# Layer 0's attention weights: GpSimd's image additions placed behind its products, score sums ordered by column tiles, the skips' matrix made with the softmax

## The chip, the core and the metric

The kernel runs on one core of a Trainium2 chip. The core has five engines with a queue of instructions each: TensorE (PE in the profile: matmuls; PEld are its weight loads), VectorE (DVE), ScalarE (ACT), GpSimd (POOL) and SyncE (SP, which here only issues DMAs). Engines wait for each other through semaphores. Operands lie in SBUF, matmul results in PSUM, both with 128 partitions; GpSimd's operands in this kernel are all in SBUF. The metric is the device time of one execution in microseconds (us); lower is better.

## The reference, cut to what matters

Two layers run on x of shape (4, 32, 128, 128): 4 batches of 32 images of 128 x 128. Layer 0, the only one touched, is a Fourier-space attention between the 32 images of a batch, with 32 heads, and two spectral convolutions behind it:

```python
k = _fno_layer(xn, Kcw, Ksw, Hs, Ws)
q = _fno_layer(xn, Qcw, Qsw, Hs, Ws)
v = _fno_layer(xn, Vcw, Vsw, H, W)
...
scores = jnp.einsum('bntk,bnsk->bnts', qf, kf) / (np.float32(np.sqrt(Hs * Ws)) * temperature)
p_attn = jax.nn.softmax(scores, axis=-1)
av = jnp.einsum('bnts,bnsk->bntk', p_attn, vf)
p = _fno_layer(av, Pcw, Psw, H, W)
a = _inorm(p + xa, attn_w, attn_b)
an = _inorm(a, norm2_w, norm2_b)
m = _fno_layer(an, m0cw, m0sw, H, W, inner_norm=True, act=True)
m = _fno_layer(m, m1cw, m1sw, H, W, inner_norm=True, act=False)
out = _inorm(m, mon_w, mon_b) + a
```

K, Q and V are spectral convolutions of one-channel images, so a head's score of two images is a weighted sum, over spectral positions, of products of the two images' spectra. The kernel makes those products once for all heads and lets TensorE weigh and sum them. `p_attn`, the probabilities, then mix the images, and `_fno_layer`'s skip terms mix them by a 32 x 32 matrix per batch (the "skips' matrix").

## The kernel before

The program is written in Tile: engines and tiles are chosen by hand, the framework puts in the semaphores and orders each engine's instructions. It does so ahead of time by a schedule of its own: program order is priority, but an instruction that its estimate takes to be ready is put ahead of one that it takes to be waiting. Tiles with the same tag share a fixed number of buffers, and a tile waits until a buffer is free. Within one PSUM bank the writes of one tile keep the order of the program.

Layer 0 loops over the 4 batches (L702). For batch b it mixes the spectra by the probabilities, works through the two convolutions, and near the end prepares batch b + 1: normalization and spectra (`image_sums`, `spectra_of_images`), then `attention_weights(b + 1, front)` (L1009). Batch 0's weights are made ahead of the loop (L648). So there are four executions of `attention_weights`, one after another in time, each followed by the mixing stage of its batch.

`attention_weights` (L489 to L595):

- The spectra `xx` of the 32 images are copied into `xe`, `xm` (SBUF) and `xp` (PSUM). TensorE sums the diagonal terms (`so`), VectorE spreads them into `sod` (L518).
- The product loop runs over 17 columns yy. Each makes `pa` and `pb`, 128 x 544 products of every image with its 16 neighbours (and itself) around the circle of 32. `pa` is always VectorE's (L534); `pb` is VectorE's in odd columns and GpSimd's in even ones (L536). TensorE multiplies them by the heads' weights (L540, L542) and sums over columns in `sp`, in four strips of 32 PSUM partitions: `pa` or `pb`, even or odd column.
- `sod`, `pa`, `pb`, and later `spt`, `ex` and `ph`, share tag `pr` with 6 buffers. The mixing stage's `u` products use the same tag.
- ScalarE copies `sp` to `spt` (L544). TensorE sums the scores `sc` in two halves of 16 images: for each half, in turn, `sod` (L552), the strips (L553), the mirrored strips (L555) and the column at distance nought (L558).
- Softmax: `mx`, `less` on VectorE, `ex` on ScalarE (L566), `sm`, `ph` on VectorE (L574). `ph` goes through DRAM (`prd`) into another layout (`pr`), by DMAs of the SP and ScalarE queues.

The main loop then makes the skips' matrix `bd` (L713 to L731): two matmuls `cm` (L718, tag `a`) of `ph` with `pv`, two products `cd` (L720, tag `v`, 3 buffers), two sums `cp` (L721), and two small operations. `pv` and `psw2` are loaded by four small DMAs and multiplied (L693 to L699), behind the loads of the two convolutions' weights.

The mixing stage (L766 to L803) loads the spectra again (`xb`, L773), copies them to PSUM on ScalarE (`xw`, L782), multiplies on VectorE (L790) and GpSimd (L788) into `u`, and sums on TensorE (`po`, L793). The skips (`pxt` L738, `sk` L757) stand between.

The end of a batch (L1010 to L1031): ScalarE scales the 32 images of `gl` (L1014). GpSimd adds `gl` to `xr` in four additions of 8 images (L1021). The inverse transform `back` (matmuls L297, evacuations into tag `v` by L187 and L189, matmuls L308) ends in VectorE's `last` (L1025), which adds to the same `xr`; `xr` is then stored (L1031). In program order this comes behind `attention_weights(b + 1)`. In time the schedule mixes the two: ScalarE's L1014 and GpSimd's L1021 run inside the product loop of batches 1 to 3.

Of the kernel before, what the change touches and what calls it, by code (L numbers as in the profile page):

```python
# [7 lines left out]
F32 = mybir.dt.float32  # L8
# [5 lines left out]
P = 128  # L14
# [94 lines left out]
def layer0(  # L109
# [67 lines left out]
    ]  # L177
    grp, small = (p.__enter__() for p in work)
    pools += work

    flip = [0]

# [303 lines left out]
    def steps(a, *dims):  # L486
        return bass.AP(tensor=a.tensor, offset=a.offset, ap=[a.ap[0], *dims])

    def attention_weights(b, front):  # L489

        xx, (xe, xm), _ = front
        xs = per_image("xs")
        nc.vector.tensor_copy(xs, xx[:, :, 0])
        half = T // 2
        nd = half + 1


        xp = ps.tile([P, 2, 512], F32, name="xp", tag="wide")
        for r in range(2):
            y0, y1 = 9 * r, min(KA, 9 * r + 9)  # L500
            nc.scalar.copy(
                xp[:, r, : (y1 - y0) * (T + half)].rearrange("p (y t) -> p y t", t=T + half), xe[:, y0:y1]
            )


        tt = [P, T, nd]
        twice = [P, 2, T]
        so = ps.tile([T, 2, T], F32, name="so", tag="wide")
        xh = per_image("xh")
        nc.vector.tensor_scalar(xh, xs, 0.5, None, ALU.mult)  # L510
        for yy in range(KA, 32):
            x_y = xx[:, :, 1 + KY + yy]
            nc.tensor.matmul(
                so, x_y, x_y.unsqueeze(1).to_broadcast(twice), start=yy == KA, stop=False
            )
        nc.tensor.matmul(so, xh, xs.unsqueeze(1).to_broadcast(twice), start=False, stop=True)
        sod = grp.tile([T, T, T], F32, name="sod", tag="pr", bufs=6)
        nc.vector.tensor_tensor(  # L518
            sod,
            ident[:T, :T].unsqueeze(2).to_broadcast([T, T, T]),  # L520
            steps(so, [1, T], [1, T]),
            ALU.mult,
        )

        sp = ps.tile([P, T, half], F32, name="sp", tag="b")
        sp0 = ps.tile([2 * NH, T], F32, name="sp0", tag="a")
        for yy in range(KA):
            row = xp[:, yy // 9, yy % 9 * (T + half) :]
            pa = grp.tile(tt, F32, name="pa", tag="pr", bufs=6)
            pb = grp.tile(tt, F32, name="pb", tag="pr", bufs=6)  # L530
            for k, t in enumerate((pa, pb)):
                other = (xm[:, yy] if k else xe[:, yy, :T]).unsqueeze(2).to_broadcast(tt)
                if k == 0 or yy % 2 == 1:
                    nc.vector.tensor_tensor(t, steps(row, [1, T], [1, nd]), other, ALU.mult)  # L534
                else:
                    nc.gpsimd.tensor_tensor(t, steps(xe[:, yy], [1, T], [1, nd]), other, ALU.mult)  # L536
            turn = dict(start=yy < 2, stop=yy >= KA - 2)
            for k, (wt, pp) in enumerate(((w_re, pa), (w_im, pb))):
                r = 32 * (2 * k + yy % 2)
                nc.tensor.matmul(sp[r : r + 32], wt[:, yy], pp[:, :, 1:], **turn)  # L540
            r = 32 * (yy % 2)
            nc.tensor.matmul(sp0[r : r + 32], w_re[:, yy], pa[:, :, 0], **turn)  # L542
        spt = grp.tile([P, 2, T, half], F32, name="spt", tag="pr", bufs=6)
        nc.scalar.copy(spt, sp.unsqueeze(1).to_broadcast([P, 2, T, half]))  # L544
        spt0 = small.tile([2 * NH, T], F32, name="spt0", tag="ym")
        nc.vector.tensor_copy(spt0, sp0)
        nn = [2 * NH, half, T]
        sc = ps.tile(nn, F32, name="sc", tag="wide")
        for h in range(2):
            i = slice(half * h, half * h + half)  # L550
            o = sc[32 * h : 32 * h + 32]
            nc.tensor.matmul(o, qk, sod[:, i], start=True, stop=False)  # L552
            nc.tensor.matmul(o[:, :, 1:nd], both_plus, spt[:, 0, i], start=False, stop=False)  # L553
            first = spt.rearrange("p r t d -> p (r t d)")[:, (half * h + nd) * half + half - 2 :]
            nc.tensor.matmul(  # L555
                o[:, :, nd:], plus_minus, steps(first, [half, half], [half - 1, half - 1]), start=False, stop=False
            )
            nc.tensor.matmul(o[:, :, 0], both_plus[: 2 * NH], spt0[:, i], start=False, stop=True)  # L558


        mx = small.tile([2 * NH, half], F32, name="mx", tag="mx")
        nc.vector.tensor_reduce(mx, sc, AX.X, ALU.max)
        less = grp.tile(nn, F32, name="less", tag="v", bufs=3)
        nc.vector.tensor_tensor(less, sc, mx.unsqueeze(2).to_broadcast(nn), ALU.subtract)
        ex = grp.tile([2 * NH, half, 2, T], F32, name="ex", tag="pr", bufs=6)
        nc.scalar.activation(ex, less.unsqueeze(2).to_broadcast([2 * NH, half, 2, T]), AF.Exp)  # L566
        sm = small.tile([2 * NH, half], F32, name="sm", tag="mx")
        nc.vector.tensor_reduce(sm, ex[:, :, 0], AX.X, ALU.add)
        nc.vector.reciprocal(sm, sm)
        ph = grp.tile([2 * NH, T, half], F32, name="ph", tag="pr", bufs=6)  # L570
        for h in range(2):
            r = slice(32 * h, 32 * h + 32)
            first = ex.rearrange("n t r d -> n (t r d)")[r, T - half * h :]
            nc.vector.tensor_tensor(  # L574
                ph[r],
                steps(first, [1, T], [2 * T - 1, half]),
                sm[r].unsqueeze(1).to_broadcast([32, T, half]),
                ALU.mult,
            )

        prd = dram.tile([2, T, 16, T], F32, name=f"prd_{b}")
        pr = big.tile([P, 4, 2, T], F32, name=f"pr_{b}", tag="prob")
        for k in range(2):
            for h in range(2):
                eng = nc.scalar if h else nc.sync
                p0 = 32 * h + 16 * k
                eng.dma_start(
                    out=prd[k, :, :, 16 * h : 16 * h + 16].rearrange("s n t -> n s t"),
                    in_=ph[p0 : p0 + 16],
                )  # L590
            eng = nc.scalar if k else nc.sync
            eng.dma_start(
                out=pr[:, :, k], in_=prd[k].rearrange("(i s) n t -> (s n) i t", i=4)
            )
        return ph, pr  # L595

    value_weights()
    normed = image_sums(0, loaded)
# [46 lines left out]
    pools.append(tc.tile_pool(name="l0_big", bufs=1))  # L645
    right.append(tc.tile_pool(name="l0_xb", bufs=4, side="right"))
    big, late = (p.__enter__() for p in (pools[-1], right[-1]))
    weights = attention_weights(0, front)  # L648


    layers = []
# [38 lines left out]
            nc.vector.memset(c0[r : r + 1, 2:4], 0.0)  # L690
        layers.append((w[:, 0], turned, (en, c0[:, 2:3]), (sq, c0[:, 3:4]), c0))

    pv = const.tile([2 * NH, 1], F32, name="pv")  # L693
    nc.sync.dma_start(out=pv[:NH], in_=heads[:, 2:3])
    nc.sync.dma_start(out=pv[NH:], in_=heads[:, 2:3])
    psw2 = const.tile([2 * NH, 1], F32, name="psw2")
    nc.sync.dma_start(out=psw2[:NH], in_=heads[:, 3:4])
    nc.sync.dma_start(out=psw2[NH:], in_=heads[:, 3:4])
    nc.vector.tensor_mul(pv, pv, psw2)  # L699


    for b in range(B):  # L702
        xt = loaded
        by_group, _, _, ysc = normed
        xd = front[2]
        if b + 1 < B:
            loaded = load(b + 1)

        ph, pr = weights

        cp = per_image("cp")  # L713
        sel = scalars(ALU.mult, "sel", same, ysc)
        for h in range(2):
            r = slice(32 * h, 32 * h + 32)
            cm = ps.tile([P, T, 16], F32, name="cm", tag="a")
            nc.tensor.matmul(cm, pv[r].to_broadcast([NH, P]), ph[r], start=True, stop=True)  # L718
            cd = grp.tile([P, T, 16], F32, name="cd", tag="v", bufs=3)
            nc.vector.tensor_tensor(cd, cm, sel.unsqueeze(2).to_broadcast([P, T, 16]), ALU.mult)  # L720
            nc.vector.tensor_reduce(  # L721
                cp[:, 16 * h : 16 * h + 16], cd.rearrange("p s t -> p t s"), AX.X, ALU.add
            )
        nc.vector.tensor_add(cp, cp, same)
        bd = small.tile([P, 4, T], F32, name="bd", tag="bd")
        nc.vector.tensor_tensor(
            bd,
            block.unsqueeze(2).to_broadcast([P, 4, T]),
            cp.unsqueeze(1).to_broadcast([P, 4, T]),
            ALU.mult,  # L730
        )  # L731
        q = big.tile([P, T, C], F32, name=f"q_{b}", tag="q")

        def skips(c0):
# [271 lines left out]
        nc.vector.tensor_mul(dg, dg, c3)  # L1006
        nc.vector.tensor_tensor(cq, cq, dg, ALU.add)
        if b + 1 < B:
            weights = attention_weights(b + 1, front)  # L1009
        for a in HALVES:  # L1010
            groups = [slice(16 * a + g, 16 * a + g + GI) for g in (0, GI)]
            for i in groups:
                for t in range(i.start, i.stop):
# [4 lines left out]
                        bias=cq[:, t : t + 1],  # L1018
                        scale=c2[:, t : t + 1],
                    )  # L1020
                nc.gpsimd.tensor_tensor(xr[:, i], xr[:, i], gl[:, i], ALU.add)  # L1021

            def last(images, four):
                for j, t in enumerate(images):
# [636 lines left out]
```

## Time and profile before

| | |
|---|---|
| median of 3 runs | 3184.4 us (3181.8 to 3186.39) |
| the profiled execution | 3176.48 us, its span 3174.4 us |
| mean granted TensorE clock | 0.954 of full |
| busy in the span | TensorE 92%, ScalarE 73%, VectorE 71%, GpSimd 65% |
| product loops of batches 0, 1, 2, 3 | 23.1, 26.4, 27.7, 27.7 us |

Times of the profile count from the span's start. A line of the timeline holds start, duration, engine, line of the program, operation, output and inputs with their shapes, how often, and in brackets the idle time of the engine just before and what ended it. In a table by stretches a number with (x) is the busy time of an engine and its instructions. "issue" is time in which an engine waited for nothing that the profile shows. TensorE takes each float32 matmul as two instructions, so counts of its rows are doubled. The end of a matmul is modelled.

### The profile page before, as it was taken

The page shows a single profiled execution, that of the slowest core. Times are in us where ns is not written, and L with a number is a line of the kernel's source. Part 1 is how long each engine was busy: PE and PEld are TensorE (multiplying, and loading weights), DVE is VectorE, ACT ScalarE, POOL GpSimd, SP SyncE. Part 2 cuts the span into 40 slices and gives each one's busy share as a digit, 9 for nine tenths or more (in the row PEclk, how much of TensorE's full clock was granted, in tenths as well). Part 3 has the DMA queues.
Part 4 walks back from the last instruction along what each step waited for, and adds up shares of the span by engine and source line. Part 5 has one row for each costly group of instructions (what it writes and reads, how often), then busy time and mean ns, then how long its engine had stood idle before and what let it go on. Part 6 is the DMA issues. An engine that isn't in the chain of part 4 may idle for free.

```text
span 3174.4 us, 52863 instructions
## 1 busy us (share of the span) xinstructions
PE 2911.8 (92%) x19530; PEld 1437.6 (45%) x19530; DVE 2257.4 (71%) x5054; ACT 2318.2 (73%) x3142; POOL 2053.0 (65%) x1819
## 2 busy tenths in 40 slices
PE   7888889798888789999999999999999999999997
PEld 4366366355446444444344444443444444444443
DVE  5776676667578557777666868866778776777887
ACT  2444343354354589998999999998999999999992
POOL 1621440350270388878888797889878889888773
PEclk8898898799798799999999999999999999999998
DMA  6401310220130201010111010021010011101000
GB/s 139 120 10 30 107 39 22 72 82 1 38 124 1 66 23 31 9 29 7 31 37 24 14 24 14 7 46 29 17 37 1 14 37 24 37 1 31 14 14 14
DMA packets 152306, 112.74 MB, mean 36 GB/s; under 512 B 36878, under 2 KB 140657, under 8 KB 151441
## 3 DMA queue, kind: packets, MB, share of 16 engines
q1 hardware_dynamic: 136209, 103.61, 12.3%
q10 hardware_dynamic: 15840, 5.77, 0.8%
q8 instruction: 154, 2.52, 0.3%
q14 instruction: 103, 0.84, 0.1%
HBM read 68.37 MB, written 20.00 MB: 28 GB/s over the span
## 4 chain that ended last, share of the span: by engine, by line
PE 62%; POOL 12%; ACT 9%; DVE 8%; issue 6%; DMA 2%; SPq 0%; POOLq 0%; DVEq 0%; ACTq 0%
PE d L1461 19%; PE po L1480 11%; PE px L1367 6%; ACT r L1511 5%; PE po L793 4%; PE n L1461 3%; POOL e L1520 3%; POOL e L1519 3%; PE pz L248 2%; PE four L308 2%; ACT e L1527 2%; PE px L886 2%; POOL kx L1126 1%; PE sk L757 1%; DVE r L1516 1%
## 5 line engine op out<-in xcount | busy, mean ns | idle before, releaser
L1516 DVE TENSOR_TENSOR r<-n,r 128x1024 f32<-128x1024 f32 (+1 forms) x1056 | 962.0, 953 | 478.3 <-PE n L1461 393.4
L1519 POOL TENSOR_TENSOR e<-r 128x512 f32<-128x512 f32 x528 | 673.0, 1275 | 268.7 <-DVE r L1516 268.1
L1511 ACT ACTIVATE r<-d 128x1024 f32<-128x1024 f32 (+1 forms) x1056 | 792.8, 802 | 68.8 <-PE n L1461 59.0
L1523 ACT ACTIVATE r<-r 128x1536 f32<-128x1536 f32 x528 | 783.6, 1484 | 16.8
L1520 POOL TENSOR_TENSOR e<-e,r 128x512 f32<-128x512 f32 x528 | 671.2, 1271 | 41.4
L1461 PE MATMUL d<-qe,ke 32*128 32x512 f32 (+3 forms) x2304 | 606.3, 602 | 39.8 <-ACT r L1511 36.5
L1480 PE MATMUL po<-e,kx 128*128 128x512 f32 (+3 forms) x1152 | 594.5, 605 | 15.7 <-POOL e L1532 15.7
L1461 PE MATMUL n<-qe,ke 32*128 32x512 f32 (+3 forms) x2304 | 606.7, 602 | 0.0
L1461 PE MATMUL n<-qf,kf 32*128 32x512 f32 (+3 forms) x2304 | 552.7, 554 | 0.0
L1461 PE MATMUL d<-qf,kf 32*128 32x512 f32 (+3 forms) x2304 | 550.3, 553 | 0.0
L1371 DVE SCALAR_TENSOR_TENSOR xc<-px,wgt,xc 128x128 f32<-128x128 f32 x1024 | 358.4, 351 | 43.0 <-PE px L1367 10.5
L1527 ACT ACTIVATE e<-e 128x512 f32<-128x512 f32 x528 | 325.8, 617 | 65.9 <-POOL e L1520 65.1
L1480 PEld LDWEIGHTS po<-e,kx 128*128 128x128 f32 x1152 | 175.5, 188 | 393.0 <-issue 308.5
L1461 PEld LDWEIGHTS d<-qe,ke 32*128 32x128 f32 x2304 | 176.5, 183 | 359.6 <-ACT r L1511 339.8
L788 POOL TENSOR_TENSOR u<-xb,gb 128x858 f32<-128x858 f32 (+1 forms) x120 | 233.5, 1968 | 156.6 <-PE po L793 110.4
L1461 PEld LDWEIGHTS d<-qf,kf 32*128 32x128 f32 x2304 | 220.4, 186 | 176.2 <-issue 164.1
L1367 PE MATMUL px<-we,x2t 128*128 128x512 f32 x512 | 265.9, 605 | 6.9 <-DVE xc L1371 5.9
L790 DVE TENSOR_TENSOR u<-xw,gb 128x858 f32<-128x858 f32 (+1 forms) x200 | 206.9, 1086 | 58.3 <-PE po L793 51.8
L1461 PEld LDWEIGHTS n<-qf,kf 32*128 32x128 f32 x2304 | 228.7, 185 | 18.9 <-issue 11.1
L900 POOL TENSOR_TENSOR spec<-part,part 128x512 f32<-128x512 f32 x16 | 24.8, 1552 | 323.7 <-DVE part L897 80.3
L793 PE MATMUL po<-u,pr 128*32 128x429 f32 (+1 forms) x1280 | 194.0, 551 | 26.3 <-DVE u L790 14.4
L1461 PEld LDWEIGHTS n<-qe,ke 32*128 32x128 f32 x2304 | 177.8, 183 | 9.2 <-DVE r L1516 0.8
(395 smaller groups left out, 3760.5 us busy)
## 6 DMA issues: line engine op xcount, KB each, us to landing
xb<-xd SPq DMA_DIRECT2D x128, 214.5 KB
xc<-x SPq DMA_DIRECT2D x29, 512.0 KB
x<-x SPq DMA_DIRECT2D x16, 512.0 KB
qf<-qe SPq DMA_DIRECT2D x64, 128.0 KB
out<-xc SPq DMA_DIRECT2D x15, 512.0 KB
xb<-xd SPq DMA_DIRECT2D x32, 198.0 KB
gb<-gd SPq DMA_DIRECT2D x4, 1056.0 KB
x<-in_x SPq DMA_DIRECT2D x8, 512.0 KB
```

The source lines that it names most:

```text
L788: nc.gpsimd.tensor_tensor(u, xb, gk, ALU.mult)
L793: nc.tensor.matmul(po[32 * j : 32 * j + 32], pr[:, i, k], u[:, r], start=i == 0 and k == 0, stop=i == 3 and k == 1,)
L1367: nc.tensor.matmul(px, x2t[:, k * P : (k + 1) * P], we[:, e0 : e0 + 4], start=True, stop=True)
L1371: nc.vector.scalar_tensor_tensor(xc[:, k], px[:, e], wgt[:, k, e0 + e : e0 + e + 1], xc[:, k], ALU.mult, ALU.add)
L1461: nc.tensor.matmul(o, k, q, start=turn == 0 or g > 0, stop=turn == 1 or g > 0)
L1480: nc.tensor.matmul(sums[c, h][:, q0 : q0 + c1 - c0], kx[:, jb], e[:, c0:c1], start=jb == 0, stop=is_last and q0 > 2 * P, skip_group_check= ...
L1511: nc.scalar.activation(r[:, g], d, AF.Ln, scale=1.0 / DSCALE)
L1516: nc.vector.tensor_tensor(r[:, g], part, r[:, g], ALU.mult)
L1519: nc.gpsimd.tensor_tensor(e, r[:, 1], r[:, 2], ALU.add)
L1520: nc.gpsimd.tensor_tensor(e, e, r[:, 0], ALU.add)
L1523: nc.scalar.activation(r, r, AF.Exp, scale=-1.0)
L1527: nc.scalar.activation(e, e, AF.Exp)
```

## The change

It has five parts.

1. Inside the main loop each of GpSimd's additions (L1021) gets an order edge, without a semaphore, behind the last product that GpSimd does for the next batch. The last batch has none.
2. `pb` is VectorE's in columns 2, 5, 8, 11 and 14, and GpSimd's in the other twelve.
3. The matmuls of the scores go step by step over both halves instead of half by half.
4. The skips' matrix is made at the end of `attention_weights`, which takes `ysc` and returns `pr`, `bd` and the last product.
5. `pv` and `psw2` are loaded and multiplied ahead of the first `attention_weights`.

```diff
+    def behind(later, earlier):
+        tc.add_manual_dep(
+            later.ins,
+            earlier.ins.name,
+            mybir.DependencyInfo(mybir.DependencyClass.NoSync, mybir.DependencyReason.DATA),
+            reason="order",
+        )
...
-                if k == 0 or yy % 2 == 1:
+                if k == 0 or yy % 3 == 2:
                     nc.vector.tensor_tensor(t, steps(row, [1, T], [1, nd]), other, ALU.mult)
                 else:
-                    nc.gpsimd.tensor_tensor(t, steps(xe[:, yy], [1, T], [1, nd]), other, ALU.mult)
+                    last_product = nc.gpsimd.tensor_tensor(t, steps(xe[:, yy], [1, T], [1, nd]), other, ALU.mult)
...
-        for h in range(2):
-            i = slice(half * h, half * h + half)
-            o = sc[32 * h : 32 * h + 32]
+        halves = [(sc[32 * h : 32 * h + 32], slice(half * h, half * h + half)) for h in range(2)]
+        for o, i in halves:
             nc.tensor.matmul(o, qk, sod[:, i], start=True, stop=False)
+        for o, i in halves:
             nc.tensor.matmul(o[:, :, 1:nd], both_plus, spt[:, 0, i], start=False, stop=False)
-            first = spt.rearrange("p r t d -> p (r t d)")[:, (half * h + nd) * half + half - 2 :]
+        flat = spt.rearrange("p r t d -> p (r t d)")
+        for o, i in halves:
+            first = flat[:, (i.start + nd) * half + half - 2 :]
             nc.tensor.matmul(
                 o[:, :, nd:], plus_minus, steps(first, [half, half], [half - 1, half - 1]), start=False, stop=False
             )
+        for o, i in halves:
             nc.tensor.matmul(o[:, :, 0], both_plus[: 2 * NH], spt0[:, i], start=False, stop=True)
...
+        (the lines of cp, sel, cm, cd and bd, moved here from the main loop)
+        return pr, bd, last_product
...
+    (the lines of pv and psw2, moved here from behind the convolutions' weights)
+    weights = attention_weights(0, front, normed[3])
...
-                nc.gpsimd.tensor_tensor(xr[:, i], xr[:, i], gl[:, i], ALU.add)
+                added = nc.gpsimd.tensor_tensor(xr[:, i], xr[:, i], gl[:, i], ALU.add)
+                if b + 1 < B:
+                    behind(added, weights[2])
```

More of the change, by code (lines that the diff above doesn't have):

```diff
@@ L487, in steps, with attention_weights @@
         return bass.AP(tensor=a.tensor, offset=a.offset, ap=[a.ap[0], *dims])
-    def attention_weights(b, front):
+    def attention_weights(b, front, ysc):
         xx, (xe, xm), _ = front
@@ L594, in attention_weights @@
             )
-        return ph, pr
+        cp = per_image("cp")
+        sel = scalars(ALU.mult, "sel", same, ysc)
+        for h in range(2):
+            r = slice(32 * h, 32 * h + 32)
+            cm = ps.tile([P, T, 16], F32, name="cm", tag="a")
+            nc.tensor.matmul(cm, pv[r].to_broadcast([NH, P]), ph[r], start=True, stop=True)
+            cd = grp.tile([P, T, 16], F32, name="cd", tag="v", bufs=3)
+            nc.vector.tensor_tensor(cd, cm, sel.unsqueeze(2).to_broadcast([P, T, 16]), ALU.mult)
+            nc.vector.tensor_reduce(
+                cp[:, 16 * h : 16 * h + 16], cd.rearrange("p s t -> p t s"), AX.X, ALU.add
+            )
+        nc.vector.tensor_add(cp, cp, same)
+        bd = small.tile([P, 4, T], F32, name="bd", tag="bd")
+        nc.vector.tensor_tensor(
+            bd,
+            block.unsqueeze(2).to_broadcast([P, 4, T]),
+            cp.unsqueeze(1).to_broadcast([P, 4, T]),
+            ALU.mult,
+        )
+        return pr, bd, last_product
     value_weights()
@@ L647, in layer0 @@
     big, late = (p.__enter__() for p in (pools[-1], right[-1]))
-    weights = attention_weights(0, front)
+    pv = const.tile([2 * NH, 1], F32, name="pv")
+    nc.sync.dma_start(out=pv[:NH], in_=heads[:, 2:3])
+    nc.sync.dma_start(out=pv[NH:], in_=heads[:, 2:3])
+    psw2 = const.tile([2 * NH, 1], F32, name="psw2")
+    nc.sync.dma_start(out=psw2[:NH], in_=heads[:, 3:4])
+    nc.sync.dma_start(out=psw2[NH:], in_=heads[:, 3:4])
+    nc.vector.tensor_mul(pv, pv, psw2)
+    weights = attention_weights(0, front, normed[3])
     layers = []
@@ L691, in layer0 @@
         layers.append((w[:, 0], turned, (en, c0[:, 2:3]), (sq, c0[:, 3:4]), c0))
[L693 to L699, printed above, removed]
     for b in range(B):
         xt = loaded
-        by_group, _, _, ysc = normed
+        by_group = normed[0]
         xd = front[2]
@@ L707, in layer0 @@
             loaded = load(b + 1)
[L709 to L731, printed above, removed]
+        pr, bd, _ = weights
         q = big.tile([P, T, C], F32, name=f"q_{b}", tag="q")
@@ L1008, in layer0 @@
         if b + 1 < B:
-            weights = attention_weights(b + 1, front)
+            weights = attention_weights(b + 1, front, normed[3])
         for a in HALVES:
```

## The prediction

> **What bounds the kernel now.** I read the chain that ended last first. Over the whole span it is mostly TensorE, with 12% on GpSimd and 8% on VectorE; that is a mean over stages.
>
> ```profile
> PE 62%; POOL 12%; ACT 9%; DVE 8%; issue 6%; DMA 2%; SPq 0%; POOLq 0%; DVEq 0%; ACTq 0%
> ```
>
> The change touches only layer 0, so I then cut out its four product loops (from the first product on VectorE to the copy of the finished sums on ScalarE) and asked for busy times in each. Columns: stretch, length, then busy time of TensorE, its weight loads, VectorE, ScalarE and GpSimd, granted clock, DMA.
>
> ```profile
> 64.10:87.20 23.10, 19.68 (x104) 5.06 (x104) 18.61 (x38) 0.00 (x0) 9.01 (x8) 0.86 0.47 82
> 304.70:331.10 26.40, 18.12 (x106) 5.64 (x106) 16.56 (x26) 10.70 (x28) 18.17 (x12) 0.81 0.05 18
> 561.00:588.70 27.70, 18.87 (x106) 5.09 (x106) 16.57 (x26) 10.74 (x28) 18.21 (x12) 0.79 0.05 16
> 820.40:848.10 27.70, 18.93 (x106) 5.12 (x106) 16.50 (x26) 10.60 (x28) 18.22 (x12) 0.79 0.05 16
> ```
>
> No engine fills these stretches: they are chains. GpSimd does 9.0 us of products in each; in batches 1 to 3 there are 9.4 us of image additions (L1021) beside them. Then the order in time, GpSimd alone, batch 0 first and batch 3 below it:
>
> ```profile
> 73.39 1.13 POOL L536 TENSOR_TENSOR pb<-xe,xm 128x544 f32<-128x544 f32 x1 [1.18 <-PE sp L540]
> 75.70 1.13 POOL L536 TENSOR_TENSOR pb<-xe,xm 128x544 f32<-128x544 f32 x1 [1.18 <-PE sp L540]
> ...
> 830.12 1.13 POOL L536 TENSOR_TENSOR pb<-xe,xm 128x544 f32<-128x544 f32 x1 [1.18 <-PE sp L540]
> 831.21 2.37 POOL L1021 TENSOR_TENSOR x<-x,g 128x1024 f32<-128x1024 f32 x1
> 833.52 1.14 POOL L536 TENSOR_TENSOR pb<-xe,xm 128x544 f32<-128x544 f32 x1
> 834.60 2.38 POOL L1021 TENSOR_TENSOR x<-x,g 128x1024 f32<-128x1024 f32 x1
> ```
>
> Batch 0 has no additions and still repeats every 2.31 us for two columns: 1.13 of product plus 1.18 of waiting for TensorE. GpSimd cannot start the next product because no buffer is free. The buffers (tag pr) are six, but `sod` keeps one: its second matmul (L552, second half) runs only after the loop, as the next view shows. With five, a GpSimd product reuses the buffer freed by the pair of columns before it, so product and matmul alternate. In batch 3 an addition of 2.37 stands between two products, and TensorE waits 2.4 us for each product so delayed.
>
> TensorE after the loop in batch 3, and VectorE and TensorE at the seam to the next stage:
>
> ```profile
> 849.17 0.62 PE L553 MATMUL sc<-spt,cst 128*32 128x256 f32 x2 [0.24 <-ACT spt L544]
> 849.62 0.97 PE L555 MATMUL sc<-spt,cst 128*32 128x240 f32 x2
> 850.52 0.23 PE L558 MATMUL sc<-spt,cst 64*32 64x16 f32 x2
> 850.68 1.04 PE L552 MATMUL sc<-sod,qk 32*32 32x512 f32 x2
> 851.65 0.62 PE L553 MATMUL sc<-spt,cst 128*32 128x256 f32 x2
> ...
> 853.01 0.23 PE L558 MATMUL sc<-spt,cst 64*32 64x16 f32 x2
> ```
>
> ```profile
> 876.14 2.16 DVE L1025 SCALAR_TENSOR_TENSOR x<-four,c,x 128x128 f32<-128x128 f32 x8 [0.25 <-PE four L308]
> 878.22 1.28 DVE L720 TENSOR_TENSOR cd<-cm,sel 128x512 f32<-128x512 f32 x2
> 879.41 1.90 DVE L721 TENSOR_REDUCE cp<-cd 128x16 f32<-128x512 f32 x2
> 881.24 1.04 DVE L790 TENSOR_TENSOR u<-xw,gb 128x858 f32<-128x858 f32 x1
> 882.33 2.36 PE L793 MATMUL po<-u,pr 128*32 128x429 f32 x10 [5.20 <-DVE u L790]
> ```
>
> The two halves of the scores run one after the other: 849.17 to 853.17, 4.0 us. And TensorE stands 5.2 us before the next stage, while VectorE makes the skips' matrix (cd, cp) ahead of the first u.
>
> **The change, part by part.** *Products, batches 1 to 3.* Removed from the loop: four additions. Moved to GpSimd: three products (12 of 17 instead of 9); VectorE has 22 instead of 25. Freed: `sod`'s buffer, because both L552 now come first and need nothing of the loop. With six buffers and two per column, a column waits for the one three before it. Per three columns: VectorE 4 x 0.64 (start to start, 830.12 to 830.76) = 2.6 us; GpSimd 2 x 1.13 = 2.3; a buffer's round is 1.13 product + 0.05 + 1.12 matmuls + 0.06 = 2.4, or 2.6 where both products are VectorE's. So 2.6 per three columns, and VectorE binds. For 17 columns that is 14.7, plus 2.0 until TensorE's first matmul (820.40 to 822.36), less what overlaps at the start. Stepped through column by column (a product starts when its engine and its buffer are free, a buffer is free when its column's matmuls end), this gives 16.3 with matmuls at full clock and 18.3 with 1.5 us of matmuls per column, as at a mixed clock. The same stepping with five buffers gives 21.7 without and 25 to 26 with additions, where the profile has 23.1 and 26.4 to 27.7, so it is about 1 us short. I take 17.4: 9.0 + 10.3 + 10.3 = 29.6 us saved. Ends: five buffers as before, or half clock throughout, give 21.0 to 21.2 (17 to 18 saved); 16.3 gives 33.
>
> A rule speaks against the new split. The Trainium skill, "GPSIMD Engine Reference", section 4.1, puts GpSimd at about twice VectorE's time for elementwise work on two inputs. The row here is 1.13 against 0.715 us, 1.6 times. By the rule a product would be 1.43, twelve of them 17.2, and GpSimd would set a loop of some 19 us; by the row they are 13.6 and VectorE's 22 x 0.64 = 14.1 bind. The row decides.
>
> *Where the additions go.* 4 x 2.36 = 9.4 us behind the last product, at about 836.5 in batch 3's times; the first two are done at 841.2, all at 845.9. VectorE's L1025 needs the first two at 862.09 now, at about 849.6 after 12.5 us are saved ahead of it. That is a slack of 8.4 us, so I cost them at nothing. ScalarE's 32 activations that feed them end at 831 already. Behind them on GpSimd are the two early u (848.19, 859.06), needed after 866. The fourth addition now falls beside ph (L574), whose two inputs are both in SBUF; section 1 of the same page says that such VectorE instructions contend with GpSimd. In the profile ph ran with GpSimd idle, so no row shows it: between 0 and 2.1 us a batch (ph's own time); I take 0.3, 1 us in all.
>
> *Scores by column tiles.* The second L552 (0.97) leaves the path; the halves write different column strips. One half alone takes 1.5 (849.17 to 850.68); halves in turn 3.0. In the product loop four strips start their first passes within 0.05 us (66.08 to 66.13), so overlap is there. I take 1.8, saving 2.2 x 3 = 6.6 (3 to 7.5). The second L552 may put the loop's first matmul 1.9 later; VectorE fills buffers meanwhile, and what shows of it is within the 17.4.
>
> *The skips' matrix.* cd and cp (1.20 + 1.83 on the chain) leave the seam, and with the sum into cp (0.18) and bd (0.28) move to right after ph, where VectorE waits for TensorE anyway (2.44 us before 862.09, 2.21 before 866.02). In batches 1 and 3 the first u comes 3.0 us earlier; in batch 2, where cd was already under a wait, 1.9. Sum 7.9. They hold two of the three v buffers that the inverse transform also needs, and one wait for cm comes ahead of evacuations on VectorE: 0.5 a batch. Net 6.4 (1 to 8). If the cover were gone, all of 3.2 would return.
>
> *Batch 0.* Its loop falls from 23.1 to about 17.4, but it isn't on the path: xd lands at 81.94, SP then issues small loads and xb, and ScalarE's `ex` (97.20) stood behind two copies of xb that landed at 96.7. If `ex` comes first in ScalarE's order, ph is ready at 90 and the path is SP's queue and the probabilities' way through DRAM; that is worth up to 7 us. If the order stays, nothing. The four loads of pv and psw (0.42 each on SP) only change places; if pv's product on VectorE stood ahead of the loop while its load stood behind xd, it costs some 7. I take +4 (-7 to +7).
>
> Sum: 29.6 + 6.6 + 6.4 + 4 - 1 = 45.6 us. The profiled execution took 3176.5 (span 3174.4, 2.1 around it), so such a one would take 3131; the median of the runs is 7.9 longer, hence 3184.4 - 45.6 = 3139. Layer 1 starts that much earlier and is otherwise as it was.
>
> **Rivals.** (1) The loop stays at 21 us: the five-buffer rhythm survives, or TensorE stays near the half clock. For it: granted clock 0.79 to 0.81 in three loops. Against: a denser loop has fewer gaps, and batch 0, denser already, got 0.86. "TensorE: Matmul & The Clock Gate", Part 1, gives about 3.4 us of sustained work to reach full clock; by it a loop without 2.4 us gaps should warm. Saved: 17.5 + 6.6 + 6.4 + 2 - 1 = 31.5, so 3153.
> (2) More than summed: batch 0 gives 7, and the inverse transform after the softmax, now at clock 0.50 (858 to 868, its four L308 at 0.95 instead of 0.53 us), runs warm, 3 us a batch: 58 saved, 3126.
> (3) Little: the order of instructions that the framework makes for the rest of layer 0 (190 us a batch between the loops) gets worse by 8 us in each batch: 3139 + 32 = 3171.
> (4) Slower: the additions come too late. Behind the last product, GpSimd's order might put the next image's u products first (1.97 us each, 30 a batch). Slack is 8.4 us; beyond it each us delays the end of the batch. It decides at 8.4 + 45.6 / 3 = 23.6 us, twelve u. At 30 us late: 3139 + 3 x 21.6 = 3204. Against: in the profile only two u precede the stage, the rest wait for TensorE's po.
>
> **How the numbers follow.** Chances: the forecast 0.53, (1) 0.24, (2) 0.11, (3) 0.07, (4) 0.05. The forecast alone spans 3129 to 3147. From 3121 to 3161 the range takes in (1) and most of (2) and leaves out (3), (4) and the low tail of (2), some 0.15. A change of 0.2%, 6.4 us, is about what measurement can tell here. Faster: the first three and most of (3), 0.93; same 0.02; slower 0.05.
>
> **What would show it.** 48 products on GpSimd and 20 of pb on VectorE; no L1021 before the last product of its batch; loops of 17 to 18 us with VectorE at its start-to-start of 0.64; 1.5 to 2 us from spt to mx; cd and cp before the last L1025; TensorE's wait for the first u near 2 us. It is wrong if the loops stay above 20 us, if L1025 waits for L1021, or if the stretches between the loops grow.

## The result, and the profile after

The changed kernel takes 3154.2 us (median of 6, 3148.26 to 3161.8) against 3179.9 us for the kernel before, run beside it (6 runs, 3169.41 to 3186.39). The ratio is 0.9926, 95% interval 0.9901 to 0.9951: 23.5 us faster, where 45.6 were forecast. The profiled execution took 3151.07 us with a span of 3149.4, which is 25.0 less than the span before; the mean granted clock is the same (0.953 and 0.954). So the two traces can be set side by side, stretch by stretch.

The chain that ended last, over the whole span, has hardly moved; layer 0 is too small a part of it to show:

```profile
PE 63%; POOL 11%; ACT 9%; DVE 9%; issue 6%; DMA 1%; SPq 0%; POOLq 0%; DVEq 0%; ACTq 0%
```

The four product loops, in the columns of the table shown of before (length, then busy time of TensorE, weight loads, VectorE, ScalarE and GpSimd, granted clock, DMA):

```profile
74.11:92.54 18.43, 18.27 (x106) 7.06 (x106) 15.79 (x38) 0.00 (x0) 11.17 (x10) 0.81 0.39 77
306.70:325.24 18.54, 18.42 (x108) 7.22 (x109) 14.15 (x23) 10.65 (x29) 12.32 (x11) 0.82 0.07 24
559.21:577.66 18.45, 18.33 (x108) 7.26 (x109) 14.14 (x23) 10.78 (x30) 12.31 (x11) 0.81 0.07 24
806.41:825.96 19.55, 19.42 (x108) 7.24 (x109) 14.24 (x23) 10.73 (x29) 12.32 (x11) 0.74 0.07 22
```

In batches 1 to 3 the loops are 8 to 9 us shorter. TensorE is now busy nearly throughout (18.42 of 18.54 us in batch 1), at a clock of 0.74 to 0.82. VectorE, in the same loop:

```profile
309.81 1.35 DVE L543 TENSOR_TENSOR pa<-xp,xe 128x544 f32<-128x544 f32 x2
313.55 0.72 DVE L543 TENSOR_TENSOR pa<-xp,xe 128x544 f32<-128x544 f32 x1 [2.39 <-PE sp L549]
```

It waits 2.39 us in one piece for TensorE, while the clock is at half; from there to the last product it works without a gap.

GpSimd at the end of the loop of batch 3 (start, duration, engine, line, operation, tiles; in brackets the idle time before it and what ended it):

```profile
817.74 4.57 POOL L545 TENSOR_TENSOR pb<-xe,xm 128x544 f32<-128x544 f32 x4 [0.73 <-PE sp L551]
822.60 2.22 POOL L545 TENSOR_TENSOR pb<-xe,xm 128x544 f32<-128x544 f32 x2 [0.29 <-DVE pa L543]
824.77 9.27 POOL L1030 TENSOR_TENSOR x<-x,g 128x1024 f32<-128x1024 f32 x4
834.01 2.69 POOL L797 TENSOR_TENSOR u<-xb,gb 128x858 f32<-128x858 f32 x1
```

Products now stand together (four in 4.57 us), and the additions follow the last one without a gap. Now the scores on TensorE, and VectorE behind them, in batch 3:

```profile
827.02 0.62 PE L562 MATMUL sc<-spt,cst 128*32 128x256 f32 x4 [0.24 <-ACT spt L553]
827.48 0.97 PE L566 MATMUL sc<-spt,cst 128*32 128x240 f32 x4
828.38 0.24 PE L570 MATMUL sc<-spt,cst 64*32 64x16 f32 x4
```

```profile
832.25 5.30 DVE L585 TENSOR_TENSOR ph<-ex,sm 32x512 f32<-32x512 f32 x2
837.58 0.69 DVE L613 TENSOR_TENSOR cd<-cm,sel 128x512 f32<-128x512 f32 x1
...
841.17 1.00 DVE L614 TENSOR_REDUCE cp<-cd 128x16 f32<-128x512 f32 x1
...
855.68 2.16 DVE L1036 SCALAR_TENSOR_TENSOR x<-four,c,x 128x128 f32<-128x128 f32 x8 [0.25 <-PE four L317]
857.75 4.02 DVE L799 TENSOR_TENSOR u<-xw,gb 128x858 f32<-128x858 f32 x4
```

```profile
858.85 0.93 PE L802 MATMUL po<-u,pr 128*32 128x429 f32 x8 [2.18 <-DVE u L799]
```

Both halves of the scores take the time of one, 1.6 us for 4.0. At the seam TensorE waits 2.18 us for the first u instead of 5.20. And one thing is new: the pair `ph` takes 5.30 us. In the trace of before it was this:

```profile
856.79 2.13 DVE L574 TENSOR_TENSOR ph<-ex,sm 32x512 f32<-32x512 f32 x2
858.96 0.69 DVE L189 TENSOR_SCALAR v<-y 128x512 f32<-128x512 f32 x1
```

Set side by side (batches 1 to 3 together, after minus before; each row is a difference of starts or ends in the two traces):

| stretch | forecast | traces | by batch |
|---|---|---|---|
| product loops | -29.6 | -25.3 | -7.9, -9.2, -8.2 |
| `spt` to `mx` (scores) | -6.6 | -7.4 | 5.17 to 2.70 each |
| the pair `ph` | +1 | +9.5 | 2.14 to 5.30 each |
| end of `ph` to the last L1036 | +1.5 | +5.5 | +2.7, +1.8, +0.9 |
| last L1036 to the first `po` | -7.9 | -10.1 | -3.0, -4.1, -3.0 |
| first `po` to the next `so` | 0 | +2.7 | +0.3, +3.7, -1.3 |
| batch 0, to its first `po` | -4 | +1.7 | 107.33 to 109.01 |

With small rests (+0.2 between `mx` and `ph`, -0.2 from `so` to the loop, -1.6 in all that follows batch 3's first `po`) the rows give -25.0, the difference of the spans. The gain was found about where it was expected; the rows that grew (`ph`, the stretch behind it, the stretch to the next `so`, batch 0) took 19.4 us of it back.

### The profile page after: what moved, and what is told of

Same layout as the page of the kernel before. It is cut to its first block, busy times and chain, and to the rows that moved or that the text cites. A ratio compares the mean times of both kernels' runs of the same rounds, so it can differ in the third digit from the quotient of the medians.

```text
span 3149.4 us, 52850 instructions
## 1 busy us (share of the span) xinstructions
PE 2907.5 (92%) x19530; PEld 1455.3 (46%) x19530; DVE 2259.2 (72%) x5042; ACT 2317.5 (74%) x3142; POOL 2069.1 (66%) x1831
## 4 chain that ended last, share of the span: by engine, by line
PE 63%; POOL 11%; ACT 9%; DVE 9%; issue 6%; DMA 1%; SPq 0%; POOLq 0%; DVEq 0%; ACTq 0%
PE d L1472 19%; PE po L1491 11%; PE px L1378 6%; ACT r L1522 4%; PE po L802 4%; PE n L1472 3%; POOL e L1530 3%; POOL e L1531 3%; PE pz L257 2%; PE four L317 2%; ACT e L1538 2%; POOL kx L1137 2%; PE sp L549 2%; PE px L895 2%; PE sk L766 1%
## 5 line engine op out<-in xcount | busy, mean ns | idle before, releaser
L1472 PEld LDWEIGHTS n<-qf,kf 32*128 32x128 f32 x2304 | 229.3, 186 | 18.7 <-issue 11.3
```

The lines of the kernel that those rows point to most:

```text
L1472: nc.tensor.matmul(o, k, q, start=turn == 0 or g > 0, stop=turn == 1 or g > 0)
```

## The experiments

Every kernel ran beside the kernel before; "saved" is one minus the ratio, times 3177 us, and the medians of before were 3176.5 to 3176.8. All of them compute the whole reference.

| kernel | median, us | ratio, 95% interval | saved, us |
|---|---|---|---|
| late half | 3151.5 | 0.9919 (0.9892 to 0.9946) | 25.7 |
| skips in the loop | 3151.2 | 0.9916 (0.9891 to 0.9941) | 26.7 |
| halves in turn | 3169.5 | 0.9979 (0.9969 to 0.9989) | 6.7 |
| every second column | 3159.2 | 0.9938 (0.9916 to 0.996) | 19.7 |
| late half and skips in the loop | 3140.8 | 0.9896 (0.9877 to 0.9915) | 33.0 |
| order alone | 3160.9 | 0.9955 (0.9941 to 0.9968) | 14.3 |
| scores alone | 3156.0 | 0.9934 (0.991 to 0.9959) | 21.0 |
| skips alone | 3180.3 | 1.0011 (0.9996 to 1.0025) | -3.5 |
| filled pause | 3139.9 | 0.9888 (0.9871 to 0.9905) | 35.6 |

**Late half.** From the changed kernel; the last two additions of a batch get a true wait for the second `ph` multiplication, which `attention_weights` returns as a fourth value:

```diff
                     behind(added, weights[2])
+                    if a == 1:
+                        behind(added, weights[3], mybir.DependencyClass.Sync)
```

> Changed kernel, but the third and fourth addition of each of batches 1 to 3 wait for ph. Theory A (GpSimd's additions slow ph, both of whose inputs lie in SBUF): the pair of ph falls from 5.30 to about 2.15 us in three batches, mx to ph's end from 8.9 to 5.7, and the time lies some 9 us below the changed kernel's 3154, near 3145. Rival B (ph is slow for another reason, as its place beside TensorE's or ScalarE's work): ph stays at 5.3 and the time at 3154. If the additions then come too late, VectorE's last adds wait for GpSimd and the inverse transform grows.

`ph` was back at 2.14, 2.13 and 2.13 us. So it is GpSimd's work beside it that stretches it: the same instructions, the same place, and only GpSimd's work moved. All executions of `ph` in the changed kernel, shortest, median and longest in ns:

```profile
L585 DVE TENSOR_TENSOR ph<-ex,sm x8: 1054/2620/2653, 99.9 to 834.9; 32x512 f32<-32x512 f32 x8
```

The 1054 is batch 0, which has no additions. The pair of batch 3 in the changed kernel, one by one, and then the first `ph` of batch 3 in "order alone" (below) with what GpSimd did beside it:

```profile
832.25 2.65 DVE L585 TENSOR_TENSOR ph<-ex,sm 32x512 f32<-32x512 f32 x1
834.92 2.62 DVE L585 TENSOR_TENSOR ph<-ex,sm 32x512 f32<-32x512 f32 x1
```

```profile
850.96 1.98 POOL L797 TENSOR_TENSOR u<-xb,gb 128x858 f32<-128x858 f32 x1
851.59 2.20 DVE L583 TENSOR_TENSOR ph<-ex,sm 32x512 f32<-32x512 f32 x1
```

Each stretched `ph` ends about 0.85 us after the GpSimd instruction that was running when it started. The fourth addition ends at 834.04 and the first `ph` at 834.89; the next stage's `u` ends at 836.71 and the second `ph` at 837.55; in "order alone" `u` ends at 852.94 and `ph` at 853.79. The additions, which had started before `ph`, kept their 2.32 us, but the `u` that started at 834.01, while the first `ph` was under way, took 2.69 us where the one after it took 2.00. So the two look as if they took turns, and a `ph` costs its own 1.05 us and most of what is left of GpSimd's instruction. Two multiplications in a row met two such instructions, an addition and a `u`.

Theory A's 2.15 us came true, its 3145 us did not: the median fell by little, 25.7 us saved against 23.5, with intervals that overlap widely. In the profiled execution, which took 3164.1 us, the inverse transform of batch 3 ran at half clock for nearly all of its length; three stretches of 3 us of it:

```profile
852.00:855.00 3.00, 3.00 (x16) 1.56 (x16) 1.80 (x7) 0.00 (x0) 0.00 (x0) 0.50 0.00 0
855.00:858.00 3.00, 3.00 (x14) 1.56 (x11) 0.27 (x1) 0.00 (x0) 0.00 (x0) 0.50 0.00 0
858.00:861.00 3.00, 3.00 (x29) 2.71 (x30) 1.13 (x4) 0.00 (x0) 0.00 (x0) 0.50 0.33 95
```

It took 28.7 us there from `ph` to the last update, where the changed kernel's took 20.3. From the first `po` to the next `so` batches 1 and 2 took 201.6 and 199.9 us as well, where the changed kernel's took 196.9 and 191.0. This execution was the slowest of the five.

**Skips in the loop.** From the changed kernel; parts 4 and 5 undone (the loads of `pv` and `psw2` go back behind the convolutions' weights):

```diff
@@ attention_weights
-        cp = per_image("cp")
-        sel = scalars(ALU.mult, "sel", same, ysc)
...
-        return pr, bd, last_product
+        return pr, ph, last_product
@@ for b in range(B)
-        pr, bd, _ = weights
+        pr, ph, _ = weights
+        ysc = normed[3]
+        cp = per_image("cp")
+        sel = scalars(ALU.mult, "sel", same, ysc)
...
```

> Changed kernel with the skips' matrix and pv back in the main loop (parts 4 and 5 undone). Theory A (the early matrix puts cm ahead of the inverse transform's matmuls and fills v buffers): from ph's end to the last L1036 the stretch returns from 19.6, 22.4, 20.3 to about 16.8, 20.6, 19.4, TensorE's wait at the seam returns from 2.2 to 5.2, together some 4 to 5 us more than the changed kernel, 3159. Rival B (the stretch grew from the late additions): it stays at 19.6, 22.4, 20.3 and only the seam is lost, 10 us, 3164. ph stays at 5.3 in both.

The seam went back to 4.04, 2.84 and 4.03 us, so 10 us of wait returned, and the time did not rise: 26.7 saved against 23.5. Neither theory had this time (3159 and 3164). In return the stretch from `ph` to the last update was 17.1, 19.2 and 18.7 instead of 19.6, 22.4 and 20.3, and batch 1's mixing was as before (192.8).

**Halves in turn.** From the changed kernel; part 3 undone, so `sod` keeps its buffer again:

```diff
-        for o, i in halves:
+        for h in range(2):
+            i = slice(half * h, half * h + half)
+            o = sc[32 * h : 32 * h + 32]
             nc.tensor.matmul(o, qk, sod[:, i], start=True, stop=False)
-        for o, i in halves:
             nc.tensor.matmul(o[:, :, 1:nd], both_plus, spt[:, 0, i], start=False, stop=False)
...
```

> Changed kernel with the scores' matmuls half by half as before (part 3 undone). Theory A (sod's buffer sets the loop's rhythm): the loops of batches 1 to 3 go from 18.5 to 21 or 22, spt to mx from 2.7 to 5.2, some 16 us more than the changed kernel, 3170. Rival B (only the additions held the loop, and buffers do not matter): loops stay at 18.5, and the time rises by 7.5 alone, 3162.

Only 6.7 us are left. Scores at 5.17 again, and the loops at 21.2, 20.9 and 20.9 us: the forecast's "five buffers as before" (21.0 to 21.2), met to 0.2. That is theory A, its 3170 us included. Here `ph` took 3.23 us: the scores are longer, the additions are over when it comes, and only the first of the two meets a GpSimd instruction, the first `u`.

**Every second column.** From the changed kernel; part 2 undone, so that VectorE has 25 products and GpSimd nine:

```diff
-                if k == 0 or yy % 3 == 2:
+                if k == 0 or yy % 2 == 1:
```

> Changed kernel with pb on VectorE in every odd column again (8 of 17), so 9 products on GpSimd (part 2 undone). Theory A (VectorE's start-to-start of 0.64 binds with six buffers): 25 x 0.64 and the lead-in, loops of 19.5 to 20.5, some 4 us more than the changed kernel, 3158. Rival B (GpSimd binds): the loops get shorter than 18.5, 3150.

Loops of 21.7, 20.1 and 17.6 us at granted clocks of 0.74, 0.83 and 1.00. The last can be compared with the loop at 1.00 shown below, 16.3 us: 1.3 us for three more products on VectorE, 0.4 each. So theory B falls; theory A's 19.5 to 20.5 us can't be separated from what the clock does to the loops. The time is 3.8 us worse than the whole change's, which the intervals don't separate.

**Late half and skips in the loop.** Both edits above together:

> The changed kernel with both suspected losses taken out together: the last two image additions of a batch wait for ph, and the skips' matrix is made in the main loop again, as before. Theory A (ph's 3.2 us a batch and the skips' cover are what ate the gain): ph pair back to 2.14 us, from ph to the last update of the images 17 to 19.5 us, TensorE's seam back to 4.0, 2.8 and 4.0, loops 18.5, from the first so to the first po 53 to 55 us a batch, time 3138 to 3146. Theory B (ph's growth lies beside other work and costs nothing): the time stays where the version with the skips in the loop was, 3150 to 3154, and the stretch from ph to the last update grows by what ph gives back.

3140.8 us, and the stretches where theory A put them, but for the loop of batch 3, which ran at full clock (16.3 us): `ph` 2.14, 2.13 and 2.13, then 17.1, 19.0 and 18.5 to the last update, seam 4.03, 2.83 and 4.03. VectorE and GpSimd in batch 3:

```profile
823.99 2.13 DVE L585 TENSOR_TENSOR ph<-ex,sm 32x512 f32<-32x512 f32 x2
826.15 0.69 DVE L198 TENSOR_SCALAR v<-y 128x512 f32<-128x512 f32 x1
```

```profile
816.51 4.68 POOL L1032 TENSOR_TENSOR x<-x,g 128x1024 f32<-128x1024 f32 x2
826.27 4.65 POOL L1032 TENSOR_TENSOR x<-x,g 128x1024 f32<-128x1024 f32 x2 [5.08 <-DVE ph L585]
```

The first evacuation `v` follows `ph` at once, and the second pair of additions starts when `ph` has ended. Against "skips in the loop" the only difference is where this pair stands. From the first `so` to the first `po` that kernel took 56.2, 57.0 and 57.8 us in batches 1 to 3, this one 53.0, 53.8 and 52.2: 3.2 or 3.3 less in each, besides the 2.3 of batch 3's loop, which ran at a higher clock. So `ph`'s growth was on the path, and theory B falls. Of the whole time 6.3 us are gained by the ratios, some 10 by the medians; the two intervals still overlap.

**Order alone, scores alone, skips alone.** The kernel before with one part each: the additions' order edge; the scores step by step over both halves; parts 4 and 5. The edits are those of the change's diff.

> The kernel before with one part alone: the additions behind the last product of their batch. Five buffers, the halves of the scores in turn, nine products on GpSimd and the skips in the main loop stay. Theory A: the loops fall to batch 0's old rhythm of 2.31 us per two columns, 22 to 23.5 us; scores stay 5.17; ph stays at 2.1 to 2.6 since the additions are done before it; 3 x 4 = 12 us saved, 3162 to 3168. Theory B (the loops were slow by TensorE's clock, not by the additions): loops 25 to 28, 3172 to 3178.

> The kernel before with one part alone: the scores' matmuls in pairs of column tiles, which also sets the sixth buffer free. The additions stay among the products. Theory A (both limits must go together): the sixth buffer helps little while a 2.4 us addition stands between two products; loops 23 to 26.5 in batches 1 to 3, 20 to 21.5 in batch 0; scores 2.7 instead of 5.17; 3155 to 3168. Theory B (the buffer was the only limit): loops 19 to 21 with the additions among the products, 3148 to 3155.

> The kernel before with one part alone: the skips' matrix made with the softmax, pv's loads and product ahead of the first loop. Loops, scores and additions stay as before. Theory A: the seam falls by 3 to 4 us a batch, but from ph to the last update it is 2 to 3 us longer and batch 1's mixing about 4 us longer, together -2 to +2 us: 3174 to 3179. Theory B (the step of the forecast holds, 6.4 us, and what ate it in the whole change is its meeting with the additions): 3168 to 3172.

The loop of batch 3 in "order alone", and then in "scores alone":

```profile
821.25:842.90 21.65, 18.29 (x106) 5.80 (x106) 16.51 (x26) 10.70 (x28) 10.15 (x9) 0.92 0.06 21
```

```profile
798.50:821.29 22.79, 19.92 (x108) 6.42 (x108) 16.41 (x26) 10.70 (x29) 18.15 (x12) 0.85 0.06 20
```

Order alone gives loops of 23.3, 21.6 and 21.7 us, and `ph` at 3.3 us, since the first `u` reaches into it (its lines stand under "late half"; the additions are over by then): 14.3 us saved, a little more than theory A's span. Scores alone gives loops of 22.7, 22.5 and 22.8 although GpSimd still has an addition between two products, and `ph` stays at 2.13, since the additions are over long before it: 21.0 us saved (13 to 29 by its interval), about what the whole change saves; its loops and scores in the trace come to 21.2. Theory A's time held, but not its claim that the sixth buffer helps little among the additions: it alone takes 3.7 to 5.2 us from a loop. Skips alone gives nothing, and its interval (0.9996 to 1.0025) leaves out the 6.4 us of the forecast's step, theory B.

Where the skips' gain goes shows in the waits of batch 1's mixing (engine, tile and line, what it waited for: us in total, times, the longest). First the changed kernel, then "skips alone", then "late half and skips in the loop":

```profile
PE po L802 <- POOL u L797: 6.7, 5, 4.6
POOL u L797 <- DMA xb<-xd: 7.8, 1, 7.8
```

```profile
PE po L800 <- POOL u L795: 6.7, 5, 4.6
POOL u L795 <- DMA xb<-xd: 7.8, 1, 7.8
```

```profile
PE po L804 <- POOL u L799: 1.6, 3, 1.0
POOL u L799 <- DMA xb<-xd: 1.5, 2, 1.3
```

In all five kernels with early skips GpSimd waits 7.4 to 8.0 us in one piece for `xb`, and TensorE 4.5 to 4.6 for GpSimd. In the five with the skips in the loop the longest wait of TensorE for that u is 1.0. SP issues the stores of the batch's images, 8.1 us of issues, ahead of the next `xb` and of the next images' loads. Before, the first `po` started 3.5 us after the last of these stores was issued (362.84 and 359.34); now 0.5 us after (357.39 and 356.92). The mixing starts earlier, the spectra do not, and so they run out.

**Filled pause.** From "late half and skips in the loop"; four matmuls of 256 columns between `so` and the loop, into `sp`, which the loop's first matmuls overwrite:

```diff
+        for _ in range(4):
+            fill = nc.tensor.matmul(sp[:NH, :16], w_re[:, 0], w_re[:, :8], start=True, stop=True)
+            behind(fill, summed)
```

> The version with the late half and the skips in the loop, and four matmuls of 256 columns more in TensorE's pause between so and the first matmul of a product loop; their result is overwritten, so nothing that is computed changes. In that version two of three loops ran at a granted clock of 0.81 to 0.82 and took 18.5 us, with TensorE busy to the end, and one ran at 1.00 and took 16.3. Theory A (TensorE's pauses ahead of the loop let the clock fall in it): loops of batches 1 to 3 at 0.95 to 1.00 and 16.2 to 16.8 us, 3134 to 3139. Theory B (when the clock falls does not hang on this pause): loops of 16.3 to 18.6 in a mixture as before, 3139 to 3145, or a little slower for the matmuls added.

The loops of batches 1 to 3 without it, and then with it:

```profile
306.86:325.31 18.45, 18.32 (x108) 7.15 (x108) 14.24 (x23) 10.64 (x28) 12.31 (x11) 0.81 0.07 24
556.32:574.90 18.58, 18.46 (x108) 7.15 (x108) 14.15 (x23) 10.78 (x29) 12.32 (x11) 0.82 0.07 25
801.43:817.70 16.27, 16.15 (x108) 7.14 (x109) 14.15 (x23) 10.62 (x29) 12.25 (x11) 1.00 0.08 27
```

```profile
304.51:321.68 17.17, 17.17 (x111) 6.10 (x109) 14.35 (x23) 10.66 (x28) 12.27 (x11) 1.00 0.08 26
551.08:569.37 18.29, 18.29 (x114) 6.55 (x112) 14.34 (x23) 10.69 (x28) 12.26 (x11) 0.97 0.07 23
799.62:816.79 17.17, 17.17 (x111) 6.10 (x109) 14.34 (x23) 10.72 (x28) 12.27 (x11) 1.00 0.08 27
```

The clock no longer falls inside a loop (batch 0: 1.00 and 17.3 us too, where it was 0.72 and 19.9); in batch 2 it was still at half when the loop began, hence 0.97. All of this is one execution; but of the twenty loops in the profiles of the five kernels with the change's scores and its additions behind the products, and no filling, only two ran at 1.00. Theory A's mechanism holds; its time does not, for the added matmuls hold up a loop by 0.9 us (17.17 against 16.27, both at 1.00), by more in batch 2, and the median moved by 0.9 us, far inside the intervals. It is the lowest median of all, by no difference that can be told.

## Why the prediction was half right

**Direction and range** held; the size was 45.6 for 23.5. The measured time lies beside the 3153 of rival (1), but not by rival (1): no loop stayed at 21 us. That the range held is in part luck, since it had been drawn wide for rival (1), and other losses filled it. (By the forecast's own loops 21.0 to 21.2 us save 18.2 to 18.8, not 17 to 18, so rival (1) belonged at 3152.) Rivals (2) and (4) did not come: in the three batches whose additions were moved, no L1036 waited for one.

**Products.** The mechanism was right, term by term: 48 products on GpSimd, no addition before the last product, six buffers instead of five (halves in turn: 20.9 to 21.2 us, forecast 21.0 to 21.2). The stepping gave 16.3 us at full clock and 18.3 at a mixed one; the runs showed 16.27 at a clock of 1.00 and 18.4 to 18.6 at 0.81 to 0.82. What was wrong was the choice of 17.4 between them: in the changed kernel all three loops ran mixed. That costs 4.3 of the 22 us missing. "So VectorE binds" holds at full clock: in the loop of 16.27 us ("late half and skips in the loop", batch 3) VectorE waits for TensorE twice before its last product, 0.25 and 0.37 us. At a mixed clock TensorE holds it up as well, 2.39 us in one piece. The clock falls when TensorE pauses ahead of the loop, which the filled pause shows. The forecast had dismissed a low clock because the denser loop would have fewer gaps: it looked for the cause inside the loop, and it lay in front of it.

**Where the additions go.** "I cost them at nothing" was right for L1036, which was looked at, and wrong for `ph`. There the forecast had 0.3 us a batch, bounded by 2.1, `ph`'s own time; it measured 3.2. This is the largest mis-sized term, 8.5 us. The bound was none: it took for granted that a `ph` can at most double, and it went to 2.5 times, for what it waits out is the rest of GpSimd's instruction, not a share of its own time. The forecast saw the fourth addition there, but not the `u` behind it, which the second `ph` met. Shown by the late half (`ph` back at 2.14) and, with the skips in the loop, in the time.

**Scores.** 1.8 us were forecast for both halves, 1.6 measured; from `spt` to `mx` 7.4 us were saved for 6.6. The order of those matmuls also set the buffer free, and alone it gives 21.0 us (13 to 29). The forecast sized six buffers only without additions, and did not see that this one edit carries most of the change.

**The skips' matrix.** The seam fell by more than the forecast's 7.9 (10.1). The step that failed is the netting: "0.5 a batch" for all that the moved work would hold up. From `ph` to the last update it cost 5.5, and the spectra's transfers took 3.6 more in batch 1 (4.6 less the 1.0 that is there anyway). That leaves about 1 us, and skips alone shows none. The cover (VectorE waiting 2.44 and 2.21 us for TensorE) was real but came too late: `cd` stands directly behind `ph`, ahead of the first evacuation of the inverse transform, on which TensorE's next matmuls wait. The first L1036 starts 5.9 us after `ph`'s end (837.55 to 843.49), where it was 3.2 (858.92 to 862.09). In three of the five kernels with early skips (late half, halves in turn, skips alone) batch 3's inverse transform then ran at a clock of 0.54 to 0.58 and took 26.9 to 28.7 us; in the five with the skips in the loop it took 17.9 to 19.2. That these go together is seen; why the clock stays low in one and not in the other is not settled.

**Batch 0.** 4 us were hoped for; the profile has 1.7 more. `ex` still stands behind copies of `xb` on ScalarE, so the order did not flip. Besides, the clock was 0.50 there during the spectra (stretch of 50 to 69 us, before and then after):

```profile
50.00:69.00 19.00, 17.17 (x125) 12.88 (x124) 11.31 (x34) 4.97 (x8) 2.01 (x2) 0.86 0.53 108
```

```profile
50.00:69.00 19.00, 18.52 (x87) 18.14 (x86) 5.95 (x17) 1.81 (x4) 0.00 (x0) 0.50 0.50 105
```

`so` came 10 us later for it, and most of that was hidden behind `xd`. Scores alone, with 0.83 there, had its first `po` at 104.06, 3.3 us before the kernel before. How much of the 5.7 us missing is the clock and how much the order stays open.

**In sum.** Of some 21 us between forecast and trace: 4.3 loops at mixed clock, 8.5 `ph`, 1.8 the net of the skips (4.6 for 6.4), 5.7 batch 0, 2.7 between batches, less 0.8 for the scores; 22.2, of which 1.6 came back in all that follows. Taking out the two that were edits, GpSimd's work beside `ph` and the early skips, gives 3140.8 us.

## What to carry to other kernels

Work that is moved behind a deadline needs two looks: what waits for it, and what it now runs beside. Here nothing waited for the moved additions, and a pair of VectorE instructions that had run with GpSimd idle lost 3 us. When a wait at a seam is filled by moving work, follow the transfers of the next stage too; the engine's wait may have covered theirs. And when a loop's chain is broken up, ask what engine then fills it and at which clock, and look for the clock's fall ahead of the loop.

## What the runs showed of the hardware that was not expected

A VectorE multiplication of two SBUF operands (32 x 512, float32) went from 1.054 to 2.62 us in the changed kernel when it started beside a GpSimd instruction, and ended about 0.85 us after that one; a GpSimd `u` that started beside it went from 2.00 to 2.69 us. The Trainium skill, "GPSIMD Engine Reference", section 1, says that the two share their SBUF interfaces and contend where VectorE has two SBUF inputs; the runs agree, and here each waited for the other's running instruction. VectorE's `mx` and `less` (0.68 each), which read the scores from PSUM, were not slowed by the additions beside them.

The clock can fall and stay low while TensorE is busy. In batch 1 of "late half and skips in the loop":

```profile
307.00:309.00 2.00, 2.00 (x12) 0.77 (x13) 1.83 (x3) 2.00 (x7) 0.00 (x0) 0.97 0.38 135
309.00:311.00 2.00, 2.00 (x10) 0.35 (x3) 1.91 (x3) 2.00 (x7) 1.12 (x1) 0.50 0.20 70
311.00:313.00 2.00, 2.00 (x9) 0.41 (x10) 0.08 (x1) 2.00 (x6) 1.13 (x1) 0.50 0.00 0
313.00:315.00 2.00, 2.00 (x15) 0.69 (x11) 1.53 (x3) 2.00 (x6) 1.13 (x1) 0.50 0.00 0
315.00:317.00 2.00, 2.00 (x20) 1.15 (x18) 1.95 (x4) 2.00 (x6) 1.31 (x2) 0.83 0.00 0
```

It fell about 2 us after TensorE's pause of 1.3 us (`so` to the first `sc`) and stayed at 0.50 for some 6.8 us of unbroken work (by the shares of 0.97 and 0.83 in the first and last row). "TensorE: Matmul & The Clock Gate", Part 1, has a free-running window of about 3.4 us, and a full idle one before the clock falls. That batch 3 kept 1.00 through the same pause fits a free-running window; that a pause of 1.3 us was enough does not fit a full idle one, and there the run decides. Why the same pause was enough in two batches and not in the third is not shown.
